# Moving the weighting, the norm's scaling, the query projections and the last two batches within the slots of a two-layer attention

## The chip, the cores and the metric

The kernel runs on one core (one NeuronCore) of a Trainium2 chip. The metric is the device time in microseconds (us) from launch to the last result, the median over several executions. The core's engines run side by side, each with an instruction queue of its own that is worked off in order: TensorE (PE in the profile; PEld is its weight load), VectorE (DVE), ScalarE (ACT), GpSimd (POOL) and SyncE (SP), whose queue here issues only DMAs. TensorE writes its products to PSUM, where the kernel has eight banks; all else lives in SBUF.

## The reference

Four layers work on `x` (8 batches x 256 channels x 512 positions), each added to its input, with a condition `cond` (8 x 512) of zeros and ones. Cut to what matters:

```python
# layer 0: masked attention, 8 heads of 32 channels, over 512 positions
q = xt @ Wq.T                                   # xt: x with the last two axes swapped
scores = scale * (qh @ qh^T)                    # keys and values are the queries too
logits = (scores * cmask + (1.0 - cmask) * NEG) * rmask     # cmask, rmask: cond by column, by row
ctx = softmax(logits) @ qh
x = x + transpose(ctx @ Wo.T)
# layer 1: modulated norm and attention, 16 heads of 32, over 256 rows of 512
scale, shift = split(cond @ W_emb + b_emb)
xn = rms_norm(x, g_norm) * (1.0 + scale) + shift
q, k, v = split(xn @ W_qkv);  q, k = rms_norm(q, g_q), rms_norm(k, g_k)
o = softmax(q @ k^T * 32 ** -0.5) @ v
x = x + (o + o @ W_out)
# layer 2: 256 steps of a fourth-order integrator, four stages each:
#          dq = q - q**3 / 3 - p + drive + tanh(q) @ coupling.T + bias
# layer 3: a gated recurrent cell (GRU) over 256 steps
```

## The kernel before

**Two stages.** `attention` (lines 25 to 577) computes layers 0 and 1 for all eight batches, and `scans` (from line 591) then runs layers 2 and 3 together, 256 steps in turn. The scans' first use of the attention's result is the first `ic` matmul (line 760), TensorE's product of `tanh(q)` and the coupling matrix. All of the change lies in `attention`.

**Slots.** The order of all work in `attention` is written out by hand (`tc.manual_schedule`, line 482): a loop over slots g, from -5 on, issues in every slot one step of each of several pipelines, and every engine does its instructions in that written order. A batch starts every U = 8 slots. In slot g

```python
b, r = divmod(g - rel, U)     # at(g, rel): the batch, and its step r of 0 to 7
```

gives what a pipeline `rel` slots deep works on. In layer 0 the 128 channels of four heads form a head group e (0 or 1), and the 512 keys four pieces kc, so step r is e = r // 4, kc = r % 4, written below as (b, e, kc). The pipelines of layer 0 are:

- `project` (line 183), at(g, -5, 2): the query projection of (b, e) into a bank `psq`; VectorE multiplies it by the mask into `qm`, ScalarE copies it to `qt` with its sum (for the mean), and one slot later `project_out` turns `qt` into `qtok`, the values, by four transposes (`ptq`).
- `scores0` (line 205), a0 = at(g, -4): four score tiles `s`, one per head, each in a bank of its own, copied to `sc` by ScalarE; `maxima0` (line 219) takes their row maxima on VectorE (2.28 us).
- `rows0` (line 225), at(g, -3) with r % 4 == 3: the maxima of (b, e) are transposed, copied to `mrow`, written by DMA to `row` in DRAM, and read back by DMA as `bc`, one value per query for all 128 partitions. Both DMAs are on SyncE's queue.
- `weights0` (line 237), e0 = at(g, 1): VectorE subtracts `bc` from `sc`; `exps0` (line 241): ScalarE's exponential of it.
- `values0` (line 245), v0 = at(g, 2): the weighted sums and the sums of weights, 2 x 4 matmuls into the two banks `pc`, over four slots; then `weigh0` (line 262): two reciprocals and two products on VectorE, which empty both banks into `ctxT`, and the masking on GpSimd (`fill`, a product, a sum).
- `masked_out` (line 276), at(g, U + 2): two projections `pso` and their addition to `x`.

Layer 1 follows at slots set per batch by the lists of lines 454 to 462: at `norms[b]` (11, 19, ..., 59 and 66) `normalize` (line 289) takes ScalarE's squares, GpSimd's `rr` and ScalarE's scaling; one slot later `modulate` (line 301) turns that by transposes (`ptx`) into `xnT`. Six parts follow, V, K and Q for two halves m (`PARTS`, line 451): `qkv` (line 316) with its bank `psqkv`, the square `sq` and the copy `qr` on ScalarE; `qkv_norm`, `qkv_out`. One part per slot, two per slot in the last two batches. The heads of layer 1 start at `HEADS[b]` (8b + 19; 65 for b = 6 and 71 for b = 7): `maxima1` (line 362, `n`), `rows1`, `weights1` (line 389), `values1` (line 413), four groups of four heads in turn. At `OUT[b]`, two slots for the two halves, `modulated_out` (line 421) makes `psx`, o @ W_out plus o, VectorE adds `x`, and one slot later `modulated_turn` (line 438) transposes the sum for the scans (`ptx2`).

**Banks.** Five of the eight PSUM banks form a ring, tag "s" (`bank`, line 60): each `bank(...)` in the written order takes the next one and waits until the tile that was in it has been read. `psq`, `ptq`, the four `s`, `pm0`, `pso`, `ptx`, `psqkv`, `n`, `s1`, `psx` and `ptx2` all share it. The other three, `c0` to `c2` (`other_bank`, line 63), hold the two `pc` of layer 0 and the sums of layer 1.

**The order around the change.** In a slot with no heads of layer 1 the order is: scores, rows, weighted sums, `project_out`, `modulated_turn`, `modulate`, subtraction, exponential, `weigh0` (in a slot whose weighted sum was kc = 3), maximum, `project`, `masked_out`, `modulation`, `normalize`, `qkv`, `modulated_out`. Slots in which heads of layer 1 run are called `late` in the code (g mod 8 in 3 to 7, from slot 19 on): there the weighted sums come last in the slot, and `weigh0` near the start of the next. The slots in which one head group's weighted sums end and the next group's first exponential runs are g = 5, 9, 13, 17, 25, 33, 41, 49 and 57 among those that are not late; the prediction calls them the switching slots.

```python
if e0 := at(g, 1, U):
    weights0(e0[0], e0[1] // 4, e0[1] % 4)
    if not late:
        exps0(e0[0], e0[1] // 4, e0[1] % 4)
if v0 and not late and v0[1] % 4 == 3:
    weigh0(v0[0], v0[1] // 4)
if a0 and a0[1] % 4 < 3:
    maxima0(a0[0], a0[1] // 4, a0[1] % 4)
```

`modulation` (line 131) computes scale and shift of layer 1 from `cond` and `W_emb`, in slots 3 to 6; `add_identity` (line 158) adds the unit matrix to `W_out`, once, at slot 8; `load_weights` (slot -1) issues the DMAs of `W_qkv` and `W_out`.

Of the kernel before, what the change touches and what calls it, by code (L numbers as in the profile page):

```python
# [8 lines left out]
F32 = mybir.dt.float32  # L9
# [15 lines left out]
def attention(ctx, tc, cst, x, cond, wqT, woT, w_emb, b_emb, g_norm, w_qkv, g_q, g_k, w_out, follow):  # L25
# [96 lines left out]
    mxp0 = [fone.tile([P, NJ, P], F32, name=f"mxp0_{i}") for i in range(2)]  # L122
    mxp1 = wp.tile([P, 2, P], F32, name="mxp1")
    for t in (*mxp0, mxp1):
        nc.vector.memset(t, 0.0)
# [5 lines left out]
    def modulation(f):  # L131

        if f == 0:
            nc.vector.tensor_scalar_mul(gqs, gq_sb, SC)
# [6 lines left out]
        pe = bank([P, 2, B], f"pe_{f}")  # L141
        for i in range(2):
            for k in range(NJ):
                nc.tensor.matmul(
                    pe[:, i, :],
                    lhsT=wemb[k][:, (f + i) * P : (f + i + 1) * P],
# [4 lines left out]
        add = vecT[:, f : f + 2].unsqueeze(2).to_broadcast([P, 2, B])  # L151
        nc.vector.tensor_tensor(ssT[:, f : f + 2, :], pe, add, ALU.add)
        if f == 6:
            nc.vector.tensor_scalar_add(G, ssT[:, 0:NJ, :], 1.0)
            nc.vector.tensor_tensor(G, G, vecT[:, 8:12].unsqueeze(2).to_broadcast([P, NJ, B]), ALU.mult)
            nc.vector.tensor_copy(shift, ssT[:, NJ:8, :])
# [24 lines left out]
    qms, qtoks, means, scs, bcs, pc0s, ctxTs = {}, {}, {}, {}, {}, {}, {}  # L181

    def project(b, e):
        if e == 0:
            qms[b] = ftwo.tile([P, 2, D], F32, tag="qm", name=f"qm_{b}")
            qtoks[b] = ftwo.tile([P, NJ, 256], F32, tag="qtok", name=f"qtok_{b}")
# [5 lines left out]
        nc.vector.tensor_mul(qms[b][:, e, :], ps, mks[b])  # L192
# [4 lines left out]
        return qt  # L197
# [7 lines left out]
    def scores0(b, e, kc):  # L205

        qm = qms[b]
        ss = [bank([P, D], f"s0_{b}_{e}_{kc}_{h}") for h in range(4)]
        for h in range(4):
            r = 32 * h  # L210
            nc.tensor.matmul(  # L211
                ss[h], lhsT=qm[r : r + 32, e, kc * P : (kc + 1) * P], rhs=qm[r : r + 32, e, :], start=True, stop=True
# [6 lines left out]
    def maxima0(b, e, qc):  # L219

        nc.vector.tensor_reduce(  # L221
            mxp0[e].rearrange("p q (h i) -> p q h i", i=32)[:, qc, :, 0], scs[b, e, qc], AX.X, ALU.max
        )

    def rows0(b, e):

        pt = bank([P, NJ, P], f"pm0_{b}_{e}")
        for qc in range(NJ):
            nc.tensor.transpose(pt[:, qc, :], mxp0[e][:, qc, :], ident)
        mrow = ftwo.tile([P, D], F32, tag="mrow", name=f"mrow0_{b}_{e}", bufs=1)  # L230
        nc.scalar.copy(mrow, pt.rearrange("p q n -> p (q n)"))
        bc = bcs[b, e] = ftwo.tile([P, 4, D], F32, tag="bc", name=f"bc_{b}_{e}", bufs=1)
# [29 lines left out]
    def weigh0(b, e):  # L262

        fill = ftwo.tile([P, D], F32, tag="fill", name=f"fill_{b}_{e}", bufs=1)
# [24 lines left out]
    def normalize(b):  # L289
# [6 lines left out]
        nc.gpsimd.tensor_tensor(rr, rr, mhalf[:, 0:2], ALU.pow)  # L296
        for m in range(2):
# [829 lines left out]
```

## Time and profile before

| | |
|---|---|
| time, median of 3 runs | 2901.79 us (2901.57 to 2904.47) |
| profiled execution, its own time | 2889.26 us |
| its span, first to last instruction | 2887.5 us |
| mean granted TensorE clock | 0.989 |
| the scans' first `ic` matmul | 825.65 us |
| TensorE busy, 0 to 187 us (ramp: the first two batches) | 148.33 us, clock 0.88 |
| TensorE busy, 187 to 640 us (steady part) | 444.92 of 453 us, clock 1.00 |
| TensorE busy, 640 to 826 us (last batches) | 169.97 of 186 us, clock 0.96 |
| TensorE busy, 826 to 2888 us (scans) | 1930.39 of 2062 us, clock 1.00 |

How to read the rows that follow. The page's first lines give each engine's busy time in us, its share of the span and its number of instructions; then the span is cut into 40 slices (72 us each), one digit a slice, the busy share in tenths, and PEclk is the granted clock of TensorE in tenths of full speed. A row of the timeline is a group of like instructions that stood together: the start in us, the duration, the engine, the line in the kernel and the operation, what it writes and reads, partitions x elements, and how many. In brackets stands how long the engine was idle ahead of it, and which engine's work on which tile and line ended that.

### The profile page before, as it was taken

Reading aid. Unit: us, or ns where it says so; the run is one execution under the profiler, and the core shown is the slowest. Engines: PE = TensorE matmul, PEld = TensorE weight load, DVE = VectorE, ACT = ScalarE, POOL = GpSimd, SP = SyncE. Lnnn points to the kernel's source line nnn. Section 1 sums busy time; section 2 is a strip of 40 time slices with the busy share of each in tenths; the row PEclk is TensorE's granted clock in tenths of the full one; section 3 lists DMA queues with packets and bytes.
Section 4 is the critical chain, followed back from the end, with each engine's and each line's share of the span. In section 5 each row is a group of like instructions: output and inputs, shape, how many; then the busy total and the mean of one; then the engine's idle time right before and its main releaser. Section 6 shows DMA issues by size and latency. Waiting matters only on the chain.

```text
span 2887.5 us, 159836 instructions
## 1 busy us (share of the span) xinstructions
PE 2693.6 (93%) x67274; PEld 1910.3 (66%) x67274; DVE 2132.2 (74%) x8986; ACT 1719.6 (60%) x8427; POOL 1091.7 (38%) x2924
## 2 busy tenths in 40 slices
PE   7799999999989999999999999999999999999998
PEld 3244444444557777777777777777777777777776
DVE  6777777675357777777777777777777777777776
ACT  5666565663346666666666666666666666666653
POOL 1134422443213444444444444444444444444442
PEclk8899999999999999999999999999999999999999
DMA  3111010101600000000000000000000000000000
GB/s 147 41 41 49 30 41 27 48 23 35 127 2 5 6 6 7 6 7 6 7 6 6 7 6 6 7 7 6 6 7 6 7 6 7 6 6 7 6 7 8
DMA packets 27559, 57.60 MB, mean 20 GB/s; under 512 B 2816, under 2 KB 17164, under 8 KB 24788
## 3 DMA queue, kind: packets, MB, share of 16 engines
q1 hardware_dynamic: 26836, 47.36, 5.3%
q8 instruction: 526, 8.62, 1.2%
q14 instruction: 197, 1.61, 0.2%
HBM read 40.15 MB, written 7.21 MB: 16 GB/s over the span
## 4 chain that ended last, share of the span: by engine, by line
PE 56%; DVE 29%; ACT 8%; issue 4%; POOL 1%; DMA 1%; ACTq 0%; SPq 0%; POOLq 0%; DVEq 0%
PE pg L795 19%; PE ic L760 18%; DVE icT L1015 5%; PE psqkv L321 5%; DVE qn L1016 5%; ACT tT L660 4%; DVE hqs L978 3%; DVE own L811 3%; PE pc L254 3%; DVE sqmm L974 2%; DVE v L813 2%; PE pc L167 2%; DVE hz L841 2%; PE s L211 2%; PE n L372 1%
## 5 line engine op out<-in xcount | busy, mean ns | idle before, releaser
L760 PE MATMUL ic<-cT_sb,tT 128*8 128x128 f32 x32736 | 1085.9, 273 | 82.4 <-ACT tT L660 44.9
L760 PEld LDWEIGHTS ic<-cT_sb,tT 128*8 128x8 f32 x32736 | 758.4, 89 | 341.4 <-ACT tT L660 269.0
L795 PE MATMUL pg<-whh_sb,hz 128*32 128x128 f32 x23904 | 795.4, 274 | 37.4 <-DVE hz L841 5.6
L660 ACT ACTIVATE tT<-qn 128x16 f32<-128x16 f32 x2046 | 441.1, 216 | 638.7 <-DVE qn L1016 537.8
L795 PEld LDWEIGHTS pg<-whh_sb,hz 128*32 128x32 f32 x23904 | 648.0, 110 | 108.5 <-DVE hz L841 108.3
L1015 DVE STREAM_TRANSPOSE icT<-ic 128x64 f32<-128x64 f32 x2048 | 503.2, 246 | 67.4 <-PE ic L760 62.8
L1016 DVE SCALAR_TENSOR_TENSOR qn<-icT,hqs 128x16 f32<-128x16 f32 x2048 | 350.6, 171 | 70.0
L755 POOL TENSOR_TENSOR W<-W,cx 128x128 f32<-128x128 f32 x765 | 297.2, 388 | 257.0 <-ACT cx L741 256.9
L748 POOL TENSOR_TENSOR W<-cx,us 128x128 f32<-128x128 f32 x255 | 116.9, 459 | 444.8 <-ACT cx L741 444.8
L974 DVE SCALAR_TENSOR_TENSOR sqmm<-sqmm,qn 128x32 f32<-128x32 f32 x768 | 153.4, 200 | 152.5 <-ACT sqmm L963 122.8
L978 DVE TENSOR_TENSOR hqs<-W,sqmm 128x32 f32<-128x32 f32 x1020 | 199.8, 196 | 46.4 <-DVE own L836 1.3
L774 PE MATMUL gi<-wih_sb,x3T 128*32 128x384 f32 (+2 forms) x3072 | 201.2, 379 | 0.0
L741 ACT ACTIVATE cx<-qn 128x32 f32<-128x32 f32 x1280 | 200.8, 213 | 0.0
L321 PE MATMUL psqkv<-wqkv_sb,xnT 128*128 128x512 f32 x384 | 174.6, 600 | 3.0 <-ACT sc L216 2.7
L221 DVE TENSOR_REDUCE mxp<-sc 128x4 f32<-128x2048 f32 x64 | 145.9, 2281 | 36.0 <-ACT sc L216 35.9
L741 ACT ACTIVATE cx<-p 128x32 f32<-128x32 f32 x1020 | 149.8, 217 | 32.2 <-DVE p L973 1.3
L216 ACT COPY sc<-s 128x512 f32<-128x512 f32 x256 | 131.5, 610 | 40.0 <-PE s L211 40.0
L239 DVE TENSOR_TENSOR sc<-sc,bc 128x2048 f32<-128x2048 f32 x64 | 147.9, 2311 | 9.2 <-DMA bc<-row 9.1
L243 ACT ACTIVATE sc<-sc,negT 128x2048 f32<-128x2048 f32 x64 | 129.0, 2018 | 35.9 <-DVE sc L239 35.9
L741 ACT ACTIVATE cx<-q 128x32 f32<-128x32 f32 x1020 | 145.6, 213 | 0.0
L963 ACT ACTIVATE sqmm<-qn 128x32 f32<-128x32 f32 x768 | 140.5, 183 | 0.8
L380 DVE TENSOR_REDUCE mxp<-n 128x2 f32<-128x512 f32 x128 | 79.5, 684 | 77.5 <-PE n L372 77.5
(165 smaller groups left out, 3385.2 us busy)
## 6 DMA issues: line engine op xcount, KB each, us to landing
bc<-row SPq DMA_DIRECT2D x16, 1024.0 KB
x<-in_x SPq DMA_DIRECT2D x8, 512.0 KB
out<-o SPq DMA_DIRECT2D x256, 16.0 KB
wqkv_sb<-in_L_cond_W_qkv SPq DMA_DIRECT2D x1, 3072.0 KB
wih_sb<-in_L_cond_W_ih SPq DMA_DIRECT2D x4, 768.0 KB
whh_sb<-in_L_cond_W_hh SPq DMA_DIRECT2D x4, 768.0 KB
x2d<-x2o SPq DMA_DIRECT2D x11, 256.0 KB
x2T<-x2d SPq DMA_DIRECT2D x11, 256.0 KB
```

The source lines that it names most:

```text
L239: nc.vector.tensor_sub(sc, sc, bcs[b, e])
L321: nc.tensor.matmul(ps, lhsT=xnTs[b][:, c, m * P : (m + 1) * P], rhs=wqkv_sb[:, c, part * D : (part + 1) * D], start=(c == 0), stop=(c == N ...
L660: nc.scalar.activation(tT, src[:, half * HM : (half + 1) * HM, :], AF.Tanh)
L741: nc.scalar.activation(c[:, i], x, AF.Copy, scale=f)
L755: nc.gpsimd.tensor_tensor(W[:, i + 1 : 5], W[:, i + 1 : 5], c, ALU.add)
L760: nc.tensor.matmul(ps[32 * j : 32 * j + B, :], lhsT=tT[k // HM][:, k % HM, :], rhs=cT_sb[:, k, j * P : (j + 1) * P], start=(k == 0), stop= ...
L774: nc.tensor.matmul(gi_ps[rows(j), g0:g1, :], lhsT=x3T[c][:, k, :], rhs=wih_sb[:, k, g0:g1, j * P : (j + 1) * P], start=(k == 0), stop=(k = ...
L795: nc.tensor.matmul(pg_ps[rows(j), :], lhsT=hzs[tau % 3][:, k, 32 * g : 32 * g + 32], rhs=whh_sb[:, k, g, j * P : (j + 1) * P], start=((k, ...
L974: stt(mm, sq, LIN[s], qs, ALU.subtract, ALU.mult)
L978: nc.vector.tensor_sub(hq, W[:, s], mm)
L1015: nc.vector.transpose(icT.rearrange("p m n -> p (m n)"), ic[:, half * 64 : half * 64 + 64])
L1016: stt(qn[:, m2, :], icT[:, :, 0:B], IC[s], hq[:, m2, :], ALU.mult, ALU.add)
```

## The change

What moves, in the diff's order:

- The maxima's tile `mxp0` becomes one tile for both head groups. The masked queries `qm` become one tile for each (b, e), three in turn. `bc` has two buffers instead of one; `mrow` and `fill` share one buffer (tag "row").
- `modulation` collects its results in one bank of tag c2 in slots 5 to 8, and its additions become one step, `scale_shift`, at slot 10; `add_identity` goes to slot 11, `load_weights` to slot 0.
- `project` is split. ScalarE's copy `qt` now stands ahead of VectorE's product with the mask, which is the new `mask`. Where a slot is not late, the projection goes ahead of the weighted sums ("queries ahead"); its mask goes behind the subtraction.
- At the start the rows of (0, 0) are issued in slot 0 behind the scores of that slot, and the scores of slot 1 are issued in slot 0 too.
- In a slot that is not late, `weigh0` goes ahead of the subtraction, and in a slot whose exponential is the first of its head group, so does one `maxima0` (`ahead`).
- `normalize` is split: squares and `rr` stay, the scaling (`normalized`) opens the next slot.
- `modulated_out` goes ahead of the `qkv` parts of its slot.
- The parts of a batch start two slots behind its norm, one for the last batch. For batches 0 to 5 nothing changes by this; for batch 6 the parts lie in slots 61 to 63 instead of 62 to 64, for batch 7 in 67 to 69 instead of 68 to 70. `HEADS` becomes 64 and 70, `OUT` (70, 71) for batch 6, and for batch 7 slot 76 holds both halves.

```diff
 
     negT = wp.tile([P, NJ, B], F32, name="negT")
     nc.vector.tensor_scalar(negT, condT, NEG, -NEG, ALU.mult, ALU.add)
-    mxp0 = [fone.tile([P, NJ, P], F32, name=f"mxp0_{i}") for i in range(2)]
+    mxp0 = fone.tile([P, NJ, P], F32, name="mxp0")
     mxp1 = wp.tile([P, 2, P], F32, name="mxp1")
-    for t in (*mxp0, mxp1):
+    for t in (mxp0, mxp1):
         nc.vector.memset(t, 0.0)
     G = wp.tile([P, NJ, B], F32, name="G")
     shift = wp.tile([P, NJ, B], F32, name="shift")
...
     def modulation(f):
 
         if f == 0:
+            cst["pe"] = other_bank([P, 8, B], "c2", "pe")
             nc.vector.tensor_scalar_mul(gqs, gq_sb, SC)
             pv = bank([P, 28], "pvs")
             nc.tensor.transpose(pv, cst["vecs"], ident[0:28, 0:28])
...
             pv = bank([P, 12], "pv")
             nc.tensor.transpose(pv, vec, ident[0:12, 0:12])
             nc.vector.tensor_copy(vecT, pv)
-        pe = bank([P, 2, B], f"pe_{f}")
-        for i in range(2):
+        for i in range(f, f + 2):
             for k in range(NJ):
                 nc.tensor.matmul(
-                    pe[:, i, :],
-                    lhsT=wemb[k][:, (f + i) * P : (f + i + 1) * P],
+                    cst["pe"][:, i, :],
+                    lhsT=wemb[k][:, i * P : (i + 1) * P],
                     rhs=condT[:, k, :],
                     start=(k == 0),
                     stop=(k == NJ - 1),
                 )
-        add = vecT[:, f : f + 2].unsqueeze(2).to_broadcast([P, 2, B])
-        nc.vector.tensor_tensor(ssT[:, f : f + 2, :], pe, add, ALU.add)
-        if f == 6:
-            nc.vector.tensor_scalar_add(G, ssT[:, 0:NJ, :], 1.0)
-            nc.vector.tensor_tensor(G, G, vecT[:, 8:12].unsqueeze(2).to_broadcast([P, NJ, B]), ALU.mult)
-            nc.vector.tensor_copy(shift, ssT[:, NJ:8, :])
+
+    def scale_shift():
+
+        nc.vector.tensor_tensor(ssT, cst["pe"], vecT[:, 0:8].unsqueeze(2).to_broadcast([P, 8, B]), ALU.add)
+        nc.vector.tensor_scalar_add(G, ssT[:, 0:NJ, :], 1.0)
+        nc.vector.tensor_tensor(G, G, vecT[:, 8:12].unsqueeze(2).to_broadcast([P, NJ, B]), ALU.mult)
+        nc.vector.tensor_copy(shift, ssT[:, NJ:8, :])
 
     def add_identity():
 
...
         nc.vector.tensor_mul(out, pc[:, 0, :], r)
 
 
     def project(b, e):
         if e == 0:
-            qms[b] = ftwo.tile([P, 2, D], F32, tag="qm", name=f"qm_{b}")
             qtoks[b] = ftwo.tile([P, NJ, 256], F32, tag="qtok", name=f"qtok_{b}")
         ps = bank([P, D], f"psq_{b}_{e}")
         for k in range(2):
             nc.tensor.matmul(
                 ps, lhsT=wq_sb[:, k, e * P : (e + 1) * P], rhs=xs[b][:, k, :], start=(k == 0), stop=(k == 1)
             )
-        nc.vector.tensor_mul(qms[b][:, e, :], ps, mks[b])
         qt = line(f"qt_{b}_{e}")
         means[b, e] = sm.tile([P, 1], F32, tag="mean", name=f"mean_{b}_{e}")
         nc.scalar.activation(qt, ps, AF.Identity, accum_out=means[b, e])
         nc.gpsimd.tensor_scalar_mul(means[b, e], means[b, e], -1.0 / D)
-        return qt
+        left["qt", b, e] = qt
+        psqs[b, e] = ps
+
+    def mask(b, e):
+        qms[b, e] = ftwo.tile([P, D], F32, tag="qm", name=f"qm_{b}_{e}", bufs=3)
+        nc.vector.tensor_mul(qms[b, e], psqs.pop((b, e)), mks[b])
 
     def project_out(b, e, qt):
         pt = bank([P, NJ, P], f"ptq_{b}_{e}")
...
 
     def scores0(b, e, kc):
 
-        qm = qms[b]
+        qm = qms[b, e]
         ss = [bank([P, D], f"s0_{b}_{e}_{kc}_{h}") for h in range(4)]
         for h in range(4):
             r = 32 * h
             nc.tensor.matmul(
-                ss[h], lhsT=qm[r : r + 32, e, kc * P : (kc + 1) * P], rhs=qm[r : r + 32, e, :], start=True, stop=True
+                ss[h], lhsT=qm[r : r + 32, kc * P : (kc + 1) * P], rhs=qm[r : r + 32, :], start=True, stop=True
             )
         sc = ftwo.tile([P, 4, D], F32, tag="sc", name=f"sc_{b}_{e}_{kc}", bufs=7)
         for h in range(4):
...
     def maxima0(b, e, qc):
 
         nc.vector.tensor_reduce(
-            mxp0[e].rearrange("p q (h i) -> p q h i", i=32)[:, qc, :, 0], scs[b, e, qc], AX.X, ALU.max
+            mxp0.rearrange("p q (h i) -> p q h i", i=32)[:, qc, :, 0], scs[b, e, qc], AX.X, ALU.max
         )
 
     def rows0(b, e):
 
         pt = bank([P, NJ, P], f"pm0_{b}_{e}")
         for qc in range(NJ):
-            nc.tensor.transpose(pt[:, qc, :], mxp0[e][:, qc, :], ident)
-        mrow = ftwo.tile([P, D], F32, tag="mrow", name=f"mrow0_{b}_{e}", bufs=1)
+            nc.tensor.transpose(pt[:, qc, :], mxp0[:, qc, :], ident)
+        mrow = ftwo.tile([P, D], F32, tag="row", name=f"mrow0_{b}_{e}", bufs=1)
         nc.scalar.copy(mrow, pt.rearrange("p q n -> p (q n)"))
-        bc = bcs[b, e] = ftwo.tile([P, 4, D], F32, tag="bc", name=f"bc_{b}_{e}", bufs=1)
+        bc = bcs[b, e] = ftwo.tile([P, 4, D], F32, tag="bc", name=f"bc_{b}_{e}")
         row = dram.tile([4, D], F32, tag="row", name=f"row_{b}_{e}", bufs=2)
         nc.sync.dma_start(row, mrow.rearrange("(h i) n -> h i n", i=32)[:, 0, :])
         nc.sync.dma_start(bc, row.rearrange("h n -> (h n)").partition_broadcast(P).rearrange("p (h n) -> p h n", h=4))
...
 
     def weigh0(b, e):
 
-        fill = ftwo.tile([P, D], F32, tag="fill", name=f"fill_{b}_{e}", bufs=1)
+        fill = ftwo.tile([P, D], F32, tag="row", name=f"fill_{b}_{e}", bufs=1)
         nc.gpsimd.tensor_scalar(fill, mks[b], -1.0, means[b, e], ALU.add, ALU.mult)
         cx = ctxTs[b][:, e, :]
         pv, pn = pc0s[b, e]
...
         rr = sm.tile([P, 2], F32, tag="rr", name=f"rr_{b}")
         nc.gpsimd.tensor_scalar(rr, ss, 1.0 / D, EPS, ALU.mult, ALU.add)
         nc.gpsimd.tensor_tensor(rr, rr, mhalf[:, 0:2], ALU.pow)
+        xhs[b] = xh, rr
+
+    def normalized(b):
+        xh, rr = xhs[b]
         for m in range(2):
             nc.scalar.activation(xh[m], xs[b][:, m, :], AF.Copy, scale=rr[:, m : m + 1])
-        xhs[b] = xh
 
...
     for b in range(B):
         per = 2 if b >= B - 2 else 1
         norms.append(U * b + U + (2 if b == B - 1 else 3))
-        start = norms[b] + (2 if b != B - 2 else 3)
+        start = norms[b] + (1 if b == B - 1 else 2)
         for i, part in enumerate(PARTS):
             parts.setdefault(start + i // per, []).append((b, *part))
         HEADS.append(start + len(PARTS) // per)
-        OUT.append((HEADS[b] + 6, HEADS[b] + (8 if per == 1 else 7)))
+        OUT.append((HEADS[b] + 6, HEADS[b] + (8 if per == 1 else 7 if b == B - 2 else 6)))
 
     def at(g, rel, n=1):
 
...
 
             a1, early = heads(g, 1, range(B - 2)), heads(g, 0, range(B - 2, B))
             late = a1 is not None or heads(g, 0, range(B - 2)) is not None
-            turns = list(leave("qkv"))
+            turns, turned = list(leave("qkv")), list(leave("qt"))
+            if g - 1 in norms:
+                normalized(norms.index(g - 1))
             if a1:
                 maxima1(*a1)
                 if v1:
                     values1(*v1)
                 if a := due.pop("weigh", None):
                     weigh0(*a)
-            elif a0:
+            elif a0 and g != 1:
                 scores0(a0[0], a0[1] // 4, a0[1] % 4)
+            if g == 0:
+                rows0(0, 0)
+                scores0(0, 1, 1)
             if (a := at(g, -3, U)) and a[1] % 4 == 3 and g > 0 and not a1:
                 rows0(a[0], a[1] // 4)
+
+            pr = at(g, -5, 2)
+            if pr and not late:
+                project(*pr)
             if v0 and not late:
                 values0(v0[0], v0[1] // 4, v0[1] % 4)
-            for a in leave("qt"):
+            for a in turned:
                 project_out(*a)
             if g == OUT[-1][1] + 1:
                 cst["soon"]()
...
                 rows0(a[0], a[1] // 4)
             if w1:
                 rows1(*w1)
-            if e0 := at(g, 1, U):
+            if v0 and not late and v0[1] % 4 == 3:
+                weigh0(v0[0], v0[1] // 4)
+
+            e0 = at(g, 1, U)
+            ahead = a0 and e0 and e0[1] % 4 == 0
+            if ahead:
+                maxima0(a0[0], a0[1] // 4, a0[1] % 4)
+            if e0:
                 weights0(e0[0], e0[1] // 4, e0[1] % 4)
                 if not late:
                     exps0(e0[0], e0[1] // 4, e0[1] % 4)
-            if v0 and not late and v0[1] % 4 == 3:
-                weigh0(v0[0], v0[1] // 4)
-            if a0 and a0[1] % 4 < 3:
+            if pr and not late:
+                mask(*pr)
+            if a0 and a0[1] % 4 < 3 and not ahead:
                 maxima0(a0[0], a0[1] // 4, a0[1] % 4)
 
-            if a := at(g, -5, 2):
-                left["qt", a[0], a[1]] = project(*a)
+            if pr and late:
+                project(*pr)
+                mask(*pr)
             if a := at(g, U + 2):
                 masked_out(a[0])
-            if 3 <= g < 7:
-                modulation(2 * g - 6)
-            if g == U:
+            if 5 <= g < 9:
+                modulation(2 * g - 10)
+            if g == U + 2:
+                scale_shift()
+            if g == U + 3:
                 add_identity()
             if g in norms:
                 normalize(norms.index(g))
+            for b in range(B):
+                for m in range(2):
+                    if g == OUT[b][m]:
+                        left["x2", b, m] = modulated_out(b, m)
             made = [(part, qkv(*part)) for part in parts.get(g, ())]
-            for b in range(B):
-                if g in OUT[b]:
-                    m = OUT[b].index(g)
-                    left["x2", b, m] = modulated_out(b, m)
-            if a0 and a0[1] % 4 == 3:
+            if a0 and a0[1] % 4 == 3 and not ahead:
                 maxima0(a0[0], a0[1] // 4, 3)
-            if g == -1:
-                rows0(0, 0)
             for part, lines in made:
                 if lines:
                     qkv_norm(*part, *lines)
...
                     due["weigh"] = v0[0], v0[1] // 4
             if (a2 := at(g, -7)) and a2[0] > 1:
                 load(a2[0])
-            if g == -1:
+            if g == 0:
                 load_weights()
             if g == U * B + 2:
                 first.close()
```

## The prediction

> **What bounds the kernel now.** I read the page first, for the shape of the span, then the timeline of TensorE alone in the attention, then all engines in one slot.
>
> ```profile
> span 2887.5 us, 159836 instructions
> PE 2693.6 (93%) x67274; PEld 1910.3 (66%) x67274; DVE 2132.2 (74%) x8986; ACT 1719.6 (60%) x8427; POOL 1091.7 (38%) x2924
> ...
> PE   7799999999989999999999999999999999999998
> ...
> PEclk8899999999999999999999999999999999999999
> ```
>
> The scans begin at 825.65 us (the first `ic` matmul behind the attention) and no line of theirs changes, so the change is worth what it moves that instant. In the attention TensorE is the bound, and it idles in two places: the ramp (slices 1 and 2) and the last two batches. From 187 to 640 us a batch takes 92.7 us (slot starts at 240.5, 333.25, 426) and TensorE has almost no gap, so whatever delays it there is paid in full.
>
> ```profile
> 94.89 1.93 PE L254 MATMUL pc<-sc,qtok 128*32 128x512 f32 x8 [8.86 <-DVE ctxT L272]
> ...
> 694.35 1.07 PE L254 MATMUL pc<-sc,qtok 128*32 128x512 f32 x8 [2.23 <-ACT sc L243]
> ...
> 818.99 0.66 PE L441 MATMUL ptx<-ident,x 128*128 128x128 f32 x4 [0.86 <-DVE x L430]
> ```
>
> The first of these waits looks like the target of the change: the weighted sums wait for `weigh0` (`ctxT`), queued on VectorE behind the subtraction. One slot of the steady part (g = 33) shows what moving it costs:
>
> ```profile
> 334.32 1.06 PE L254 MATMUL pc<-sc,qtok 128*32 128x512 f32 x8
> 335.20 1.04 PE L254 MATMUL pc<-sc,ones 128*32 128x512 f32 x8
> 335.52 2.28 DVE L239 TENSOR_TENSOR sc<-sc,bc 128x2048 f32<-128x2048 f32 x1
> 336.17 3.70 PE L321 MATMUL psqkv<-wqkv_sb,xnT 128*128 128x512 f32 x8
> 337.72 1.75 DVE L271 RECIPROCAL r<-pc 128x256 f32<-128x256 f32 x1
> 337.84 2.00 ACT L243 ACTIVATE sc<-sc,negT 128x2048 f32<-128x2048 f32 x1 [1.38 <-DVE sc L239]
> 339.71 3.60 PE L425 MATMUL psx<-wout_sb,oT 128*128 128x512 f32 x8
> 339.91 0.60 ACT L334 ACTIVATE sq<-psqkv 128x512 f32<-128x512 f32 x1
> 340.41 0.58 ACT L336 COPY qr<-psqkv 128x512 f32<-128x512 f32 x1
> 341.97 2.28 DVE L221 TENSOR_REDUCE mxp<-sc 128x4 f32<-128x2048 f32 x1
> 343.68 2.35 PE L211 MATMUL s<-qm 32*128 32x512 f32 x8
> 344.16 0.68 DVE L430 TENSOR_TENSOR x<-psx,x 128x512 f32<-128x512 f32 x1
> 345.95 0.64 PE L254 MATMUL pc<-sc,qtok 128*32 128x512 f32 x4
> ```
>
> To be seen: VectorE runs subtraction (335.52), `weigh0` (337.72 to 341.97, 4.25 us), maximum. ScalarE's queue is exponential, square, copy, and the last two empty the bank of `psqkv`. Five banks rotate; the next slot's four score groups (343.68) need the banks of `psqkv` and `psx`. The scores take 2.27 us to the next row where 1.07 is usual: the bank of `psx` comes free at 344.84.
>
> **The change, part by part.** Sums are against the profiled execution's own 2889.26 us (span 2887.5); the runs' median, 2901.79, lies 12.5 us or 0.43% above it. I add the shift to the median.
>
> *1. `weigh0` and one maximum ahead of the subtraction, steady part.* In g = 25, 33, 41, 49, 57 VectorE will run weigh (4.25), maximum (2.19), subtraction (2.2). At g = 33: last weighted matmul done 336.24, weigh 336.3 to 340.55, maximum to 342.75, subtraction from there; the exponential follows a subtraction's start by 2.32 (335.52 to 337.84), so 345.07; the copy `qr` ends 3.15 behind an exponential's start (337.84 to 340.99), so 348.2. In the changed order `psx` goes ahead of `psqkv`, which therefore has the bank of the fourth score group. That group can start at 348.2 where it now starts at 344.84. The loss is 3.4 us a slot: TensorE's queue is in order, and the weighted sums, `ptx`, `pso` stand behind it. The exponential itself (done 347.1) is then in time. Five slots: +17.2. GpSimd's share of `weigh0` (fill, product, sum) comes earlier and hides; so do the shared row buffer (fill starts 338.70, the row's DMA was issued at 327.86) and its other side (sum done 344.75, next row copy 372.87).
>
> *2. The same at g = 17.* There is no `psx`, so less work covers the chain: weighted sums done 154.28, then 4.25 + 2.19 + 2.32 + 3.15 gives 166.3 for the fourth score group, now free at 159.1: +7.2. TensorE then idles 7 us, so its clock drops. In the trace the 16 matmuls behind the 8.86 us gap took 3.57 us, other such groups 1.86: +1.7. Together +8.9.
>
> *3. Ramp.* "Queries ahead" puts ScalarE's `qt` before the mask (first scores 0.7 us later, at 10.8), but lets the second projection go before the transposes; the first row copy is ready at about 25.1 (now 26.39), as the last maximum ends at 24.45, and the first weighted sums start at 36.6 (now 37.86). Nothing else on SP is moved past: the row, its broadcast and the two weight loads keep their order, and two `bc` buffers take a wait from later broadcasts. With the query projections done early, the fourth weighted sum of (0,0) ends at about 56.0 (now 61.7): a lead of 5.7 us. Then weigh, maximum, subtraction and exponential stand in a row: 4.25 + 2.19 + 2.32 + 2.07 = 10.9, and the next weighted sums start at 67.0 (now 66.27). The lead is gone. Modulation matmuls (g = 5 to 8 instead of 3 to 6) only fill that wait; dropping three additions of 0.17 us is nothing.
> At g = 10 the chain is again 85.2 + 10.9 = 96.1 (now 94.89, where the broadcast landed at 88.2 and `weigh0` followed it): +1.3. Additions into `x`, the next subtraction and exponential and the squares come later by as much, the scaling then starts at 114.2 (now 113.08), and nothing stands between squares and scaling in ScalarE's queue, so the slot's delay hides no wait for `rr`. At g = 12 the query projection, now ahead of the weighted sums, waits for a bank that ScalarE frees behind this scaling (116.0); the weighted sums (1.86) that ran in the gap now follow it. Transposes, `xnT` and the exponential behind them end at 126.7, so the weighted sums of g = 13 start there (now 121.1): +5.6. They end at 128.6; the chain of 10.9 gives 139.5 for the next (now 130.47), +9.1, with a half-clock stretch of 1.7 behind it: about +10.5 at g = 15. TensorE is full from there to g = 17, so nothing is won back.
>
> *4. Half clock in the five steady slots.* The row first: gaps of 2.36 us (ahead of 130.47) and 2.23 (ahead of 694.35) left the next 16 matmuls at full speed, the gap of 8.86 did not. The Trainium skill, "TensorE: Matmul & The Clock Gate", Part 1, states that TensorE falls to half rate after an idle window of about 3.4 us and needs about as long a busy one to recover. It speaks against a change that merges small waits into long ones. My gaps are about 3 us, broken by a score group: by the skill 0, by the row of the long gap 1.7 each, 8.5 in all. I take 0.3 each, +1.5, nearer the rows of 2.3 us.
>
> *5. The norm's scaling one slot later.* In the steady part ScalarE no longer waits for `rr` (2.10 us at 364.42) ahead of `qT` and an exponential; TensorE's first key-query products lost 0.35 us to that `qT` (1.42 for 1.07). Six batches: -2. What is late next is `ptx`, which needs the scaling and a bank.
>
> *6. Last two batches.* Q, K and V of batch 6 move from g = 62 to 64 into 61 to 63, batch 7's from 68 to 70 into 67 to 69. The work stays; what goes is stalls. Now `n` and `ptx` lose 0.56 + 1.75, `pso` and `s` 1.48 + 1.71 + 0.96 between 711 and 727. With `pc` and the weighted sums laid between, I count the first weights of batch 6 done 9 us earlier. At g = 67 about 2.8 us goes back: the scaling of batch 7 waits behind four exponentials of 0.6, and Q, K, V of that slot need its transposes, which `psx` (3.43) just covers. At the end both `psx` groups go back to back, and the 1.12 + 0.5 of the first one's addition and transposes is hidden: -1.6. Sum -8.
>
> Sum: 10.5 + 8.9 + 17.2 + 1.5 - 2 - 8 = +28.1 us. Operations whose durations no row of before shows: none; only the places are new.
>
> **The rivals.**
> - *Faster: the broadcast comes late anyway.* If in the switching slots `bc` lands later than 6.4 us (weigh and maximum) behind the last weighted sum, weighing first is free, parts 1 and 2 vanish and the ramp keeps its 5.7 us: -5.7 - 2 - 8 = -16, 2886 us. For it: at g = 9 it landed 3.3 us behind, and the wait of 8.86 us names `ctxT`. Against: at g = 33 subtraction did not wait at all, and a lead in the ramp brings maxima and row earlier too. Chance 0.12.
> - *The ramp half as bad.* If the walk of part 3 misplaces the g = 12 bank wait (5 us) and the clock stays up there and at g = 17 (3.4): +19, 2921 us. Chance 0.18.
> - *The last two batches win nothing* (scaling at g = 67 and the exponentials collide, and the long gap drops the clock): +36, 2938 us. Chance 0.13.
> - *Half clock in all five steady slots*: +7 more, 2937 us. Chance 0.12.
> - *The parts cancel*, the tail winning twice what I count and the ramp losing nothing: within 0.2% of before. Chance 0.06.
>
> **How the numbers follow.** My forecast, +28, has the remaining 0.39: 2901.8 + 28 = 2930 us, own range 2922 to 2937. Cases below 2907 are the faster one and most of the cancelling one, 0.17; above 2946 lie the tail and clock rivals together, about 0.03. So 2907 to 2946. About 0.2% (6 us) is what a measurement of this kernel can tell from no change. Faster 0.12, same 0.06, slower 0.82.
>
> **What would show it.** Right: in each switching slot `sc<-sc,bc` starts about 6.5 us behind the last `pc`, the next score group takes over 5 us from its start to the following `pc`, and the batch grows from 92.7 to about 96; around g = 13 a gap of 5 to 6 us ahead of `pc` with the clock at 0.5; the first `ic` at about 854 us instead of 825.65. Wrong: the subtraction's row names the DMA as its releaser; the period stays 92.7; or the slots around 115 to 140 us are not longer.

## The result, and the profile after

The changed kernel takes 2942.23 us (median; 2940.13 to 2944.81) against 2901.68 us before (2893.28 to 2904.47): the ratio is 1.0145, 95% interval 1.0123 to 1.0167, so it is 1.45% slower, +40.5 us by the medians. The forecast was +28 us, 2930, range 2907 to 2946. The kernel before was measured again beside each group of experiments, with medians of 2896.05, 2898.88 and 2896.77; against the first of these the change costs 46 us. Ratios below are to the runs of before on the same chip; the medians of before in these groups differ by up to 6 us.

The page of the changed kernel, first lines:

```profile
span 2940.9 us, 159857 instructions
PE 2719.2 (92%) x67274; PEld 1916.6 (65%) x67274; DVE 2136.0 (73%) x8982; ACT 1720.0 (58%) x8427; POOL 1082.1 (37%) x2924
...
PE   7789999999998999999999999999999999999998
...
PEclk8899999999999999999999999999999999999999
```

The number of matmuls is the same, yet TensorE is busy for 25.6 us more (2719.2 against 2693.6). For the most part this is a lower clock, as shown below: part of the loss hides inside "busy", and the list of idle gaps alone would miss it. The page's clock digits are too coarse to show it.

Where the time went is read from anchors that both traces have, rows of VectorE and TensorE. In the kernel before:

```profile
219.86 1.28 DVE L380 TENSOR_REDUCE mxp<-n 128x2 f32<-128x512 f32 x2
...
270.42 0.69 DVE L430 TENSOR_TENSOR x<-psx,x 128x512 f32<-128x512 f32 x1 [2.81 <-POOL qr L346]
...
639.73 0.69 DVE L430 TENSOR_TENSOR x<-psx,x 128x512 f32<-128x512 f32 x1 [2.46 <-issue]
...
825.65 1.90 PE L760 MATMUL ic<-cT_sb,tanh 128*8 128x128 f32 x32 [1.12 <-DVE ic L668]
```

And in the changed kernel:

```profile
242.38 1.88 DVE L387 TENSOR_REDUCE mxp<-n 128x2 f32<-128x512 f32 x3
...
299.76 0.69 DVE L437 TENSOR_TENSOR x<-psx,x 128x512 f32<-128x512 f32 x1 [2.03 <-POOL qr L353]
...
693.92 0.69 DVE L437 TENSOR_TENSOR x<-psx,x 128x512 f32<-128x512 f32 x1 [2.46 <-issue]
...
880.81 1.06 PE L784 MATMUL ic<-cT_sb,tanh 128*8 128x128 f32 x32 [0.98 <-DVE ic L692]
```

The differences are 22.5, 29.3, 54.2 and 55.2 us. So the stages of the two profiled executions are:

| stage | forecast, us | measured, us |
|---|---|---|
| ramp, with g = 17 | 10.5 + 8.9 = 19.4 | 22.5 |
| steady part, five switching slots | 17.2 + 1.5 - 2 = 16.7 | 31.7 |
| last two batches | -8 | +1.0 |
| first `ic` matmul | 28.1 | 55.2 |

A batch takes 99.0 us in the steady part (374.15 to 473.11, two additions of `psx` a batch apart) instead of 92.7 (344.16 to 436.88), that is 6.3 us per switching slot. (The profiled execution of before was 12 us below its median, so the trace's difference is larger than that of the medians.)

The slot g = 33 of the changed kernel and what follows it, timeline of TensorE, VectorE and ScalarE, answers to the rows shown of before (in a row of scores, x2 is the product of one head):

```profile
361.98 1.14 PE L215 MATMUL s<-qm 32*128 32x512 f32 x8
...
363.93 1.04 PE L258 MATMUL pc<-sc,ones 128*32 128x512 f32 x8
364.90 3.70 PE L432 MATMUL psx<-wout_sb,oT 128*128 128x512 f32 x8
365.04 1.76 DVE L275 RECIPROCAL r<-pc 128x256 f32<-128x256 f32 x1 [0.71 <-PE pc L258]
...
369.30 2.28 DVE L225 TENSOR_REDUCE mxp<-sc 128x4 f32<-128x2048 f32 x1
371.49 2.73 DVE L243 TENSOR_TENSOR sc<-sc,bc 128x2048 f32<-128x2048 f32 x1
...
372.40 1.13 PE L215 MATMUL s<-qm 32*128 32x512 f32 x4
374.15 0.68 DVE L437 TENSOR_TENSOR x<-psx,x 128x512 f32<-128x512 f32 x1
374.26 2.00 ACT L247 ACTIVATE sc<-sc,negT 128x2048 f32<-128x2048 f32 x1 [9.07 <-DVE sc L243]
374.88 1.12 PE L215 MATMUL s<-qm 32*128 32x512 f32 x2 [1.35 <-DVE x L437]
...
376.64 0.57 ACT L343 COPY qr<-psqkv 128x512 f32<-128x512 f32 x1
...
377.27 2.07 PE L215 MATMUL s<-qm 32*128 32x512 f32 x2 [1.27 <-ACT qr L343]
...
379.27 1.94 PE L258 MATMUL pc<-sc,qtok 128*32 128x512 f32 x8
...
380.98 1.93 PE L258 MATMUL pc<-sc,ones 128*32 128x512 f32 x8
382.85 1.12 PE L448 MATMUL ptx<-ident,x 128*128 128x128 f32 x4
```

This is the forecast chain, link by link: weighing (365.04 to 369.3), maximum, subtraction (371.49), exponential (374.26), the copy `qr` (376.64), and only then the fourth score matmul (377.27), whose releaser is named, `qr`. The subtraction starts 6.5 us behind the last weighted sum; about 6.5 was forecast. Then look at the durations. The weighted sums behind that take 1.94 and 1.93 us, where before they took 1.06 and 1.04. That is the clock, as the windows of TensorE in the same slot say (busy time and count, granted clock, DMA share, GB/s):

```profile
375.00:377.00 2.00, 1.00 (x2) 1.00 0.00 0
377.00:379.00 2.00, 1.73 (x2) 0.55 0.00 0
379.00:381.00 2.00, 2.00 (x12) 0.50 0.00 0
381.00:383.00 2.00, 2.00 (x13) 0.50 0.00 0
383.00:385.00 2.00, 2.00 (x7) 0.75 0.00 0
```

From about 377.2 to 384 TensorE ran at half speed: 6.8 us, which cost some 3.4. The fourth score product starts 12.3 us behind the weighted sums instead of 8.6, a delay of 3.7; the two together give about 7. The batch grew by 6.3 against before, and by 6.9 against the first kernel of the next section, which has all of the change but this order and takes 92.1 us a batch. Of the delay only 1.35 + 1.27 us are idle time. The rest is one more group of scores. All four heads take 1.14 us side by side in the row at 361.98; before, the scores of this slot came in two groups (2.35 us at 343.68), here they come in three, of 1.1 us and more each.

### The profile page after: what moved, and what is told of

Same layout as the page of the kernel before. It is cut to its first block, busy times and chain, and to the rows that moved or that the text cites. A ratio compares the mean times of both kernels' runs of the same rounds, so it can differ in the third digit from the quotient of the medians.

```text
span 2940.9 us, 159857 instructions
## 1 busy us (share of the span) xinstructions
PE 2719.2 (92%) x67274; PEld 1916.6 (65%) x67274; DVE 2136.0 (73%) x8982; ACT 1720.0 (58%) x8427; POOL 1082.1 (37%) x2924
## 3 DMA queue, kind: packets, MB, share of 16 engines
q14 instruction: 197, 1.61, 0.2%
## 4 chain that ended last, share of the span: by engine, by line
PE 57%; DVE 28%; ACT 8%; issue 4%; POOL 1%; ACTq 0%; DMA 0%; SPq 0%; POOLq 0%; DVEq 0%
PE pg L819 19%; PE ic L784 18%; DVE icT L1039 5%; PE psqkv L328 5%; DVE qn L1040 5%; PE pc L258 4%; ACT tT L684 4%; DVE hqs L1002 3%; DVE own L835 3%; DVE sqmm L998 2%; PE s L215 2%; DVE v L837 2%; PE pc L168 2%; DVE hz L865 2%; PE s L402 1%
## 5 line engine op out<-in xcount | busy, mean ns | idle before, releaser
L215 PE MATMUL s<-qm 32*128 32x512 f32 x512 | 116.0, 669 | 27.5 <-ACT qr L343 13.5
```

The costliest lines, as they stand in the source:

```text
L215: nc.tensor.matmul(ss[h], lhsT=qm[r : r + 32, kc * P : (kc + 1) * P], rhs=qm[r : r + 32, :], start=True, stop=True)
```

## The experiments

**Is the order on VectorE the cause at all?** Two kernels, one from each side. The changed kernel with the old order there:

```diff
-            if v0 and not late and v0[1] % 4 == 3:
-                weigh0(v0[0], v0[1] // 4)
...
-            ahead = a0 and e0 and e0[1] % 4 == 0
+            ahead = False
...
                     exps0(e0[0], e0[1] // 4, e0[1] % 4)
+            if v0 and not late and v0[1] % 4 == 3:
+                weigh0(v0[0], v0[1] // 4)
```

> The changed kernel with weigh0 and the maximum back behind the subtraction and exponential in every slot; queries ahead, norm's scaling, two bc buffers and the last two batches stay as changed. Chain theory (weighing and maximum delay the exponential, it delays the copy that frees the fourth score group's bank, and TensorE's clock halves behind that): the five steady switching slots give back 6.3 us each (31.6) and the ramp with g = 17 gives back its 22.5 and the lead of the queries, so 2942 becomes 2880 to 2895. Rival (the order of the banks, psx ahead of psqkv, or the early query projections cost the time): at most 10 us come back, 2930 or more.

And the kernel before with the new order alone:

```diff
-            if e0 := at(g, 1, U):
+            if v0 and not late and v0[1] % 4 == 3:
+                weigh0(v0[0], v0[1] // 4)
+            e0 = at(g, 1, U)
+            ahead = a0 and e0 and e0[1] % 4 == 0
+            if ahead:
+                maxima0(a0[0], a0[1] // 4, a0[1] % 4)
+            if e0:
                 weights0(e0[0], e0[1] // 4, e0[1] % 4)
...
-            if v0 and not late and v0[1] % 4 == 3:
-                weigh0(v0[0], v0[1] // 4)
-            if a0 and a0[1] % 4 < 3:
+            if a0 and a0[1] % 4 < 3 and not ahead:
...
```

> The kernel before with one edit: weigh0, and the maximum of a switching slot, ahead of the subtraction. Chain theory: the five steady slots lose about 6 us each (30), the ramp and g = 17 between 10 and 25, so 2942 to 2955. Rival (psx ahead of psqkv is needed for the loss): the fourth score group keeps its bank, and the kernel stays within 10 us of before, 2912 or less.

Measured: 2893.4 us with the order undone (ratio 0.9984, interval 0.9976 to 0.9992), 2946.02 us with the order alone (1.0167, 1.0150 to 1.0184). So this one part carries the whole loss, and all other parts together win 0.16%. In the first kernel's trace a batch takes 92.1 us. The order of the banks (`psx` ahead of `psqkv`) isn't needed for the loss: the second kernel has the old order of these two, and its batch takes 99.1 us.

**Weighing or maximum?** The changed kernel with `ahead = False`, nothing else:

> The changed kernel with only the maximum of the switching slots back behind the subtraction; weigh0 stays ahead. Chain theory: the chain is 2.2 us shorter, the fourth score group is late by 1.5 us instead of 3.7 and the clock stays up, so about 4.8 us in each of five slots and about 8 in the ramp and g = 17: 2905 to 2915. Rival (the weighing ahead of the subtraction is what costs, the maximum is hidden): 2930 or more.

Measured: 2916.57 us (1.0072, 1.0057 to 1.0088), a little above the range expected; a batch takes 93.9 us on average. TensorE behind the switching slots g = 33 and g = 41 of this kernel:

```profile
358.90 1.13 PE L215 MATMUL s<-qm 32*128 32x512 f32 x4
360.93 1.31 PE L215 MATMUL s<-qm 32*128 32x512 f32 x4 [0.90 <-DVE x L437]
362.17 1.50 PE L258 MATMUL pc<-sc,qtok 128*32 128x512 f32 x8
...
453.62 1.13 PE L215 MATMUL s<-qm 32*128 32x512 f32 x4
455.65 1.32 PE L215 MATMUL s<-qm 32*128 32x512 f32 x4 [0.90 <-DVE x L437]
456.90 1.07 PE L258 MATMUL pc<-sc,qtok 128*32 128x512 f32 x8
```

The wait for `qr` is gone. At g = 25, 41 and 57 the weighted sums are at full speed; at g = 33 and 49 the clock still fell, for 3.4 us each (362.66 to 366.08 in the first), although the rows ahead of it and the gap of 0.90 us are the same. So 2.2 us taken out of the chain bring back 5.1 us per batch (99.0 to 93.9): about half is the chain, the other half the clock, which was at 0.50 for 6.8 us in every one of these slots and is now for 1.4 on average.

**The clock by itself.** Work for TensorE in the two waits behind each of the five steady switching slots, nothing moved:

```diff
+        fl = other_bank([P, D], "c2", f"fl_{b}_{e}_{kc}") if fills else None
         for h in range(4):
             r = 32 * h
+            if fills and h > 1:
+                nc.tensor.matmul(fl, lhsT=ident, rhs=wq_sb.rearrange("p k e -> p (k e)"), start=True, stop=True)
...
-                scores0(a0[0], a0[1] // 4, a0[1] % 4)
+                scores0(a0[0], a0[1] // 4, a0[1] % 4, fills=g in (26, 34, 42, 50, 58))
```

> The changed kernel with two matmuls of 128x512 added whose result nobody reads (0.86 us each, the unit matrix by the weights, into the idle bank c2), ahead of the third and of the fourth score matmul in the slot behind each of the five steady switching slots: work for TensorE in the two waits of 1.3 us, nothing else moved. Clock theory (6.6 us at half clock behind the waits cost 2.3 to 3.3 us a slot, and the clock stays up if the waits are filled): 11 to 16 us faster than the changed kernel, 2926 to 2931. Rival (the loss is the wait alone, or the clock falls anyway): 2939 or more.

Measured: 2927.47 us (1.0107, 1.0087 to 1.0126), 14.8 us less than the changed kernel by the medians and 11 by the ratios, with ten matmuls more. TensorE behind the switching slot g = 41 (`fl` is the added work), and its windows:

```profile
464.37 1.13 PE L217 MATMUL fl<-wq_sb,ident 128*128 128x512 f32 x2
465.79 1.12 PE L218 MATMUL s<-qm 32*128 32x512 f32 x2 [0.29 <-DVE x L440]
466.84 1.13 PE L217 MATMUL fl<-wq_sb,ident 128*128 128x512 f32 x2
468.18 1.12 PE L218 MATMUL s<-qm 32*128 32x512 f32 x2 [0.21 <-ACT qr L346]
469.23 1.07 PE L261 MATMUL pc<-sc,qtok 128*32 128x512 f32 x8
```

```profile
466.00:468.00 2.00, 1.97 (x4) 1.00 0.00 0
468.00:470.00 2.00, 1.82 (x10) 1.00 0.00 0
470.00:472.00 2.00, 2.00 (x17) 1.00 0.00 0
```

The releasers are the same and the waits end where they did; only the clock stays at 1.00, in all five slots, and the batch takes 95.7 us instead of 99.0. The half clock is therefore worth 3.2 us per switching slot, shown apart from the wait.

**Ramp and steady part apart.** The changed kernel with the new order only up to slot 17, and only from slot 18 on (the two conditions with `g < 18` or `g >= 18`, the old place for the other slots):

> The changed kernel with weigh0 and the maximum ahead of the subtraction up to slot 17 only. If the costs add up by stage: 2942 minus five slots at 6.6, 2909; the shift at the first psx addition stays near 22 us and the batch takes 92.1 us. Rival (no cost in the ramp, where the broadcast lands late anyway): 2893 to 2897.

> The changed kernel with weigh0 and the maximum back behind the subtraction up to slot 17, and ahead of it from slot 18 on. If the costs add up by stage: the run with everything back (2893.4) plus five slots at 6.6 us, 2926; per batch 99.0 us against 92.1. Rival (the ramp's lag is what starves the steady slots, so without it they recover): 2905 or less.

Measured: 2910.42 us (1.0044, 1.0029 to 1.0059) and 2921.39 us (1.0083, 1.0063 to 1.0102). Above the ratio of the kernel with the order undone (0.9984), that is 0.60% and 0.99%, or 17 and 29 us; their sum, 46, is what the order costs in all (1.0145 - 0.9984 = 1.61%, 47 us). The stages add. The steady one is a little below the forecast of the experiment (2926).

**The last two batches alone**, in the kernel before, with `modulated_out` ahead of the `qkv` parts:

```diff
-        start = norms[b] + (2 if b != B - 2 else 3)
+        start = norms[b] + (1 if b == B - 1 else 2)
...
-        OUT.append((HEADS[b] + 6, HEADS[b] + (8 if per == 1 else 7)))
+        OUT.append((HEADS[b] + 6, HEADS[b] + (8 if per == 1 else 7 if b == B - 2 else 6)))
...
```

> The kernel before with one edit: Q, K, V, heads and outputs of the last two batches one slot sooner, modulated_out ahead of the qkv parts. By the prediction's step 6: -8 us, 2894. Rival from the changed trace (from 54.2 us behind at the last steady slot to 55.1 at the first ic matmul: the tail gave nothing): 2900 to 2904.

Measured: 2891.58 us (0.9981, 0.9973 to 0.9989), 4.5 us less by the medians. Between the last steady addition and the first `ic` lie 181.4 us (before 185.9, changed kernel 186.9). So the move does win, and something else in the change takes it away again. TensorE of the changed kernel at g = 67:

```profile
789.09 0.33 PE L316 MATMUL ptx<-ident,xh 128*128 128x128 f32 x1 [2.65 <-ACT xh L306]
```

The transposes `ptx` of the last batch wait 2.65 us for its norm's scaling, which stands behind ScalarE's four exponentials in the next slot. Undone for that batch alone, in the kernel with the old order:

```diff
-            if g - 1 in norms:
+            if g - 1 in norms[:-1]:
                 normalized(norms.index(g - 1))
...
                 normalize(norms.index(g))
+                if g == norms[-1]:
+                    normalized(B - 1)
```

> The run with weighing and maximum back behind the subtraction, and in it the norm's scaling of the last batch back in its own slot (66), ahead of the four exponentials that it waited behind. By the trace, ptx waited 2.65 us for that scaling and the clock halved behind it: 3 to 4.5 us less than 2893.4, so 2889 to 2890.5. Rival (the wait moves to the next link): 2892 or more.

Measured: 2890.27 us (0.9972, 0.9959 to 0.9985). The wait is gone from its trace:

```profile
732.28 1.25 PE L316 MATMUL ptx<-ident,xh 128*128 128x128 f32 x8
```

and the stretch from the last steady addition to the first `ic` falls from 188.8 us (old order alone) to 182.7. By the ratios this is 0.12%, 3.5 us; the two intervals overlap, so the trace carries this reading more than the times do.

The clock has a share in these stretches that must be taken off first. In the stretch of the kernel with the old order half clock takes 10.2 us, in that of the kernel with the new order from slot 18 on 5.1, though in this stretch both do the same work in the same order (what it takes is one less the granted clock, summed over the stretch). Without it, the stretch is 179.1 us before, 176.3 with the move alone, 178.0 to 178.8 in the six kernels with the move and the late scaling, and 175.3 to 175.9 in the three that have the last scaling back in its slot (this one and the next two). So the move wins some 2.8 us, and the late scaling of the last batch takes about as much back, its wait of 2.65 us.

**What the other two parts are worth.** From the kernel with the old order, the scaling back in its slot in all batches; and from the kernel just shown, the projections back behind the weighted sums:

> The run with weighing and maximum back behind the subtraction, and in it the norm's scaling back in the slot of its squares in all eight batches. The prediction's step 5 gave the split 2 us in six batches (0.33 each), and the last batch's split costs 2.65 us or more: if both hold, about 2 us above the run in which only the last batch's scaling is back, 2892. Rival (the split wins nothing in the steady part): 2890, the same as that run.

> The run with the last batch's scaling back in its own slot, and in it the query projections back behind the weighted sums in every slot. If the queries' lead is eaten by the broadcasts of slots 9 and 13 and by the bank wait of slot 12, as the ramp's rows say (first psx addition at 252.8 us against 251.4 before): the same within 3 us, 2887 to 2893. Rival (the early queries carry the lead of 5.7 us to the end): 2895 or more.

Measured: 2887.22 us (0.9967, 0.9955 to 0.9979) and 2889.12 us (0.9972, 0.9961 to 0.9982). Neither part shows a gain in the times: without the delayed scaling the kernel is not slower, nor without the early queries. (The trace without the early queries reaches the first `ic` 6.6 us sooner, 815.58 against 822.17, but its execution lay 5.3 us below the median of its runs, so nothing follows from that.) The first of these is the fastest kernel of the study by its median, 0.33% faster than before and 1.8% faster than the changed one, though it can't be told from the two beside it.

## Why the prediction was right, point by point

- **Step 1, the chain in the steady slots: right.** Forecast 12.0 us from the last weighted sum to the fourth score group (336.24 to 348.2), measured 12.3 (364.9 to 377.2, the matmul's end to the next start); forecast loss 3.4 (348.2 less 344.84, which for five slots is 16.8 and not 17.2), measured 3.7. The difference is the subtraction, which took 2.73 us here instead of 2.28. One wait became two, for `psx`'s addition and for `qr`, since both stand behind the chain.
- **Step 4, half clock in these slots: mis-sized by ten.** 0.3 us a slot was taken, 3.2 measured (16 instead of 1.5 in five slots). The step reasoned that gaps of about 3 us broken by a score group stay near the rows of 2.3 us that left the clock up. The gaps were 1.35 and 1.27 us, shorter still, with one score matmul of 1.12 us between, and yet the clock fell. So the longest gap does not decide. In the 3.41 us ahead of each of the five drops (373.79 to 377.20 in this slot) TensorE worked for 1.12 us; how little work is too little, the runs do not show (last section). The rule of the Trainium skill ("TensorE: Matmul & The Clock Gate", Part 1: half rate after an idle window of about 3.4 us), read as one unbroken gap, also gave 0; the trace decides against that reading. The rival with half clock in all five slots (+7 us) had the right mechanism, at half its size.
- **Steps 2 and 3, ramp and g = 17: right within 3 us.** 22.5 measured for 19.4. Some 2 us of the difference are there from the start: the first weighted sums begin at 38.46 where the walk had 36.6. The chain of 10.9 us appears as forecast. TensorE of the changed kernel:

```profile
99.69 1.94 PE L258 MATMUL pc<-sc,qtok 128*32 128x512 f32 x8 [10.27 <-ACT sc L247]
...
117.21 3.26 PE L189 MATMUL psq<-x,wq_sb 128*128 128x512 f32 x4 [2.00 <-ACT sc L220]
...
142.49 1.94 PE L258 MATMUL pc<-sc,qtok 128*32 128x512 f32 x8 [6.15 <-ACT sc L247]
...
181.25 2.07 PE L215 MATMUL s<-qm 32*128 32x512 f32 x2 [7.16 <-ACT qr L343]
```

  Each of the waits that the walk named is there with its releaser: the exponential at g = 10 and g = 14, the bank of the early projection at g = 12, `qr` behind g = 17. From the end of the weighted sums to the next ones it takes 11.3 us (88.35 to 99.69). One wait isn't in the walk: at 67.61 a score product waits 5.70 us for VectorE's copy `vecS` of the modulation, queued behind the subtraction. It costs little, as the exponential of that slot ends at 69.43 and the weighted sums start at 69.61. The half-bad ramp is refuted.
- **Step 5, the scaling one slot later: no gain shown by the times.** Forecast -2; undoing it everywhere left the time where it was or lower. In the traces, the one steady batch that no late broadcast touched takes 92.37 us with the scaling back in its slot everywhere, against 92.10 with it delayed: 0.3 us, as forecast for a batch, but too little for the times to show.
- **Step 6, the last two batches: the direction right, the size not.** Forecast -8 with 2.8 us given back at g = 67. The give-back is the one of the trace (2.65 us of wait). The gain ahead of it was counted too high: the move by itself wins 4.5 us by the medians, 2.8 in the trace without the clock's share, instead of some 11. Together next to nothing was left, as the rival "win nothing" (+8 us) had it.
- The sum: the two rivals just named happened together, which by their own figures is 28 + 7 + 8 = 43 us. In the traces the first `ic` is even 55 us later, but the profiled execution of before lay 12.5 us below its median; the medians differ by 40.5. The measured 2942 us is inside the stated range, but outside the forecast's own one of 2922 to 2937. The direction and the chain were foreseen; that the size stayed inside, with two terms wrong in the same direction, was in part luck. The prediction gave these two together about 0.03 and put them above 2946, where its own figures make 2945.

That the steady part's error is the clock, and not a further wait, is shown by the filled kernel. The runs of before spread over 16 us (2888.5 to 2904.8 in 42 runs), and this goes with the clock too: the twelve with a mean granted clock of 0.988 or more took 2888.5 to 2898.3 us, the eleven with 0.984 or less 2899.8 to 2904.8. Why an execution is granted more or less is not settled; what the traces offer is told below.

## What to carry to other kernels

Before moving a consumer ahead of a wait, follow what stands behind it in the same queue: here 6.5 us of VectorE work went ahead of a subtraction whose data had long been there, and the exponential, a copy and a bank stood behind that subtraction. In a trace, compare an engine's busy time for the same number of instructions: most of TensorE's +25.6 us with no matmul more was the halved clock (some 16 in the five steady slots alone), and two waits of 1.3 us delayed the scores by 3.7 us and cost 3.2 us more behind them. When two traces differ by a few us, take off first what the clock cost in each. A step put one slot later is free only in those slots where nothing long stands ahead of it in the new place.

## What the runs showed of the hardware that was not expected

- Two idle gaps of 1.35 and 1.27 us within 3.7 us halved TensorE's clock for 6.8 us. Two matmuls laid into the gaps kept it at 1.00.
- In the attention of all twelve traces the granted clock is 1.00 or 0.50, and it changes only at points of a grid 3.41 us apart, which lies differently in each execution. In the changed kernel it fell at 278.20, 377.20 and 476.18 us and rose at 285.04, 384.02 and 483.00, all whole multiples of 3.4135 us apart. So a stretch at half clock lasts 3.4 us or a multiple of it and costs busy TensorE 1.7 us each time. This is also how slots that look alike can differ: in the kernel with only the maximum moved back, the clock fell in two of five. What decides at a point of the grid stays open: there, 2.51 us of busy time in the 3.41 us before it were too little once (ahead of 362.66) and enough once (ahead of 645.97).
- A slightly late broadcast can come before a loss of this kind in the old order. In the kernel with the last two batches moved, one steady slot (g = 41) had it:

```profile
433.49 2.90 DVE L239 TENSOR_TENSOR sc<-sc,bc 128x2048 f32<-128x2048 f32 x1 [0.41 <-DMA bc<-row]
...
443.49 1.24 PE L211 MATMUL s<-qm 32*128 32x512 f32 x4 [1.21 <-DVE x L430]
...
444.66 1.94 PE L254 MATMUL pc<-sc,qtok 128*32 128x512 f32 x8
```

  A wait of 0.41 us for the DMA and a longer subtraction ended in 1.21 us of idle TensorE and in weighted sums at half clock, for 3.4 us. The run with the scaling back in all batches had such a wait in two slots, and half clock behind one of them. This and the place of the grid would fit the spread of the runs of before, but no run here tests either.
- The subtraction of a steady switching slot took 2.73 us in the changed kernel and 2.28 in the one before, on the same data. In the traces of these two and of the kernel with the last batches moved, every subtraction of layer 0 that took 2.6 us or more ran beside one of GpSimd's two operations on `fill`, which belong to `weigh0` (0.59 us of overlap at 371.49); beside GpSimd's other work it took 2.28. No run moves `fill` alone, so the cause is not shown.
